# A fused attention and FFN kernel: how the second square layer's weight sums are fetched, summed and stored

## The chip, the core and the metric

The kernel runs on one core of one Trainium2 chip. The metric is device time in microseconds, lower is better. The engines are named as in the profile: PE (TensorE), DVE (VectorE), ACT (ScalarE), POOL (GpSimd) and SP (SyncE, which here only issues DMAs). "L846" is line 846 of the kernel before.

## The reference

x has the shape 2 x 2048 x 256. With a causal softmax attention of one head and a gated FFN of two square layers of 1024:

```python
xn = layernorm(x)
attn = softmax(causal(xn@Wq @ (xn@Wk).T) / 16) @ (xn@Wv) @ Wo
h = silu(xn@w1.T * s1) * (xn@w2.T * s2)     # 256 -> 1024
h = gelu(h@h1.T * sh1)                      # 1024 -> 1024, the first square layer
h = gelu(h@h2.T * sh2)                      # 1024 -> 1024, the second square layer
out = x + attn + h@w3.T * s3                # 1024 -> 256
```

All is float32. The FFN's weights are -1, 0 or 1 in the inputs; the kernel looks at them at run time and takes a branch of its own for such weights.

## The kernel before

The kernel has two parts. The first 280 us compute the attention and, beside it, examine the weights. Its results and the normalized, transposed x are stored to DRAM (`r_d`, `xT_d`). Then `ffn_ternary` works through N = 8 blocks of 512 rows in pairs, n = 0, 2, 4, 6.

Each square layer is a product of 1024 x 1024 weights with a pair of blocks of 1024 rows, done by a scheme of seven products of half size in place of eight (`STEPS`). Each step has a weight factor and an activation factor: step 0 is A11 with B11, step 1 S1 with T1, step 2 S2 with T2, step 3 S4 with B22, step 4 S3 with T3, step 5 A12 with B21, step 6 A22 with T4. The A are quarters of the weights; the S are sums of quarters. In the names of the code, S1 = a21 + a22, S2 = S1 - a11, S4 = a12 - S2 and S3 = a11 - a21.

A factor is a DRAM slab of 1 MB (`factors["h1"]` and `factors["h2"]`, seven slabs each, in the order of the steps). `fetch_factors` (L949) loads one into one of three SBUF buffers (pool `wpt`, on SP) as soon as a buffer is free, so that a factor is asked for two steps ahead of its use. `product` (L846) then runs 32 matmuls of 128 x 128 x 512.

The first layer's sums are made in the attention part. The second layer's are made in the FFN part, once, during the first pair (n = 0), by `make_h2(c)` for four chunks c = 0 to 3: two fetches of 512 KB on POOL's DMA queue (L915) into two tiles of the tag `stg`, four subtractions or additions of 128 x 512 on POOL (`sums_of_factors`, L151) into the one tile of the tag `sums` (`bufs=1`), and a store of 1 MB on POOL's queue (L919). `copy_h2` (L928, SP) copies the three plain quarters from DRAM to DRAM. `load_w3` fetches and rounds the last weights in two halves (L923, L132), in tiles of the tag `stg`. Where these calls stand is told by the dictionary `later`: names ("B11", "B21", ...) are quarters of the gated layer, numbers are steps of the first square layer:

```python
later = {
    "B11": lambda: make_h2(0), "B21": lambda: make_h2(1), "B12": lambda: copy_h2(0),
    0: lambda: copy_h2(5), 1: lambda: make_h2(2), 2: lambda: copy_h2(6),
    3: lambda: make_h2(3), 5: lambda: load_w3(0), 6: lambda: load_w3(SC // D),
}
```

`rests_of(n)` loads the attention's results (L962) and x (L963) of both blocks and adds them on POOL (L964); the outputs go into the same tiles and from there to DRAM (L999). x uses the tag `sums`, the two rests use the tag `stg`, one tile each.

The text's order is a priority only: the program is built with `schedule_with_timeline_sim=True`, a planner that gives each engine its order by a simulated timeline and adds the waits. On the chip each engine, and each queue of DMA issues (SP's, POOL's, ACT's), then runs in that fixed order.

Other lines that are named below: L170 the gated layer's products, L178 and L179 its activation (ACT) and scaling (DVE), L183 and L184 the split of an activation factor into two parts (ACT and DVE), L821, L826 and L827 the sums that make T1, T3 and T2 (DVE, POOL, DVE), L885 the sum for T4 (POOL), L866 and L867 the sums behind the products and their Gelu, L767 the loads of x.

Of the kernel before, what the change touches and what calls it, by code (L numbers as in the profile page):

```python
# [9 lines left out]
F32 = mybir.dt.float32  # L10
# [5 lines left out]
ALU = mybir.AluOpType  # L16
# [4 lines left out]
P = 128  # L21
TB = 512
NT = TB // P
# [13 lines left out]


STEPS = [("A11", "B11"), ("S1", "T1"), ("S2", "T2"), ("S4", "B22"), ("S3", "T3"), ("A12", "B21"), ("A22", "T4")]
LOW_BITS = 0xFFF  # L40


# [20 lines left out]
def attn_ffn_kernel(  # L63
# [35 lines left out]
    nc = tc.nc  # L99
    B, S, D = x.shape  # L100
# [4 lines left out]
    HC = H // P  # L105
    SC = 1024
# [15 lines left out]
    HB = H // 2  # L122
    HK = HC // 2
    factors = {k: dram.tile([P, len(STEPS), HK, HB], F32, name=f"factors_{k}") for k in ("h1", "h2")}

# [4 lines left out]
    def rounded(dst, src):  # L130

        nc.gpsimd.tensor_scalar(dst, src, 1.0, 0.0, ALU.mult, ALU.add)  # L132

    def rows_of(n):
        return x[n // NB, ds((n % NB) * TB, TB), :].rearrange("(t p) d -> p t d", p=P)
# [4 lines left out]
    def sums_of_factors(sums, halves, which, engine=nc.gpsimd):  # L140

        (a11, a21), (a12, a22) = ((t[:, :HB], t[:, HB:]) for t in halves)
        done = sums.bitcast(F32) if sums.dtype == F32R else sums
        for i in which:
            x, y, op = (
                (a21, a22, ALU.add),
                (done[:, 0, :], a11, ALU.subtract),
                (a12, done[:, 1, :], ALU.subtract),
                (a11, a21, ALU.subtract),
            )[i]  # L150
            engine.tensor_tensor(sums[:, i, :], x, y, op)  # L151
# [35 lines left out]
    with ExitStack() as actx:  # L187
        cp = actx.enter_context(tc.tile_pool(name="cp", bufs=1))
        stgp = actx.enter_context(tc.tile_pool(name="stgp", bufs=2))
# [360 lines left out]
        def low(tiles, dst):  # L550
# [4 lines left out]
            with tc.issue_after(marks["DVE"]):  # L555
                nc.vector.tensor_scalar(tb, tb, LOW_BITS, None, ALU.bitwise_and)
            with tc.issue_after(marks["ACT"]):
# [11 lines left out]
        sums = xh0.rearrange("p c h t -> p (c h) t")  # L569
# [180 lines left out]
    def ffn_ternary(actx):  # L750
# [4 lines left out]
        stgp = actx.enter_context(tc.tile_pool(name="stgpt", bufs=2))  # L755
# [6 lines left out]
        w3_sb = fw.tile([P, HC, D], F32R, name="w3_sbt")  # L762
        xh1 = fw.tile([P, DC, 2, TB], F32R, name="xh1t")

        def load_xh(n):
            t = xh1 if n % 2 else xh0
            nc.sync.dma_start(out=t.bitcast(F32).rearrange("p c h t -> p (c h t)"), in_=xT_d[n])  # L767
# [64 lines left out]
        def square(layer, n, B, sets, last, beside):  # L832
# [6 lines left out]
            def product(step, out, start):  # L839
                right = STEPS[step][1]  # L840
                fetch_factors()
                w = factor_tiles.pop(0)
                for o in range(HK):
                    for c in range(HK):
                        for a in range(2):
                            nc.tensor.matmul(  # L846
                                out=out[o], lhsT=w[:, c, ts(o, P)], rhs=sets[right][c][:, a, :],
                                start=(start and c == 0 and a == 0), stop=(c == HK - 1 and a == 1),
                                skip_group_check=True,
                            )  # L850
                if step in beside:
                    beside.pop(step)()
# [55 lines left out]
                    t2(C, nxt, name, i)  # L908
            return C, nxt

        def make_h2(c):
            halves = []
            for k in (c, c + HK):
                t = stgp.tile([P, SC], F32, tag="stg", name=f"stgt_h2_{k}")
                nc.gpsimd.dma_start(out=t, in_=h2[:, k, :])  # L915
                halves.append(t)
            sums = stgp.tile([P, 4, HB], F32, tag="sums", name=f"sums_h2_{c}", bufs=1)
            sums_of_factors(sums, halves, range(4))
            nc.gpsimd.dma_start(out=factors["h2"][:, 1:5, c, :], in_=sums)  # L919

        def load_w3(c):
            t = stgp.tile([P, SC], F32, tag="stg", name=f"stgt_w3_{c}")
            nc.gpsimd.dma_start(out=t, in_=w3[:, c : c + SC // D, :].rearrange("p c d -> p (c d)"))  # L923
            rounded(w3_sb[:, c : c + SC // D, :].rearrange("p c d -> p (c d)"), t)

        def copy_h2(step):
            k, o = {0: (0, 0), 5: (HK, 0), 6: (HK, HB)}[step]
            nc.sync.dma_start(out=factors["h2"][:, step], in_=h2[:, ds(k, HK), ds(o, HB)])  # L928

        later = {
            "B11": lambda: make_h2(0), "B21": lambda: make_h2(1), "B12": lambda: copy_h2(0),
            0: lambda: copy_h2(5), 1: lambda: make_h2(2), 2: lambda: copy_h2(6),
            3: lambda: make_h2(3), 5: lambda: load_w3(0), 6: lambda: load_w3(SC // D),
        }
        assert HK == 4 and HC == 2 * SC // D


        factor_order = [  # L940
            (layer, n, step) for n in range(0, N, 2) for layer in ("h1", "h2") for step in range(len(STEPS))
        ]
        factor_tiles = []

        def fetch_factors():
            while factor_order and len(factor_tiles) < 3:
                layer, n, step = factor_order.pop(0)
                w = wp.tile([P, HK, HB], F32R, tag="w", name=f"w_{layer}_{n}_{STEPS[step][0]}")
                nc.sync.dma_start(  # L949
                    out=w.bitcast(F32).rearrange("p c o -> p (c o)"),  # L950
                    in_=factors[layer][:, step].rearrange("p c o -> p (c o)"),
                )
                factor_tiles.append(w)

        def rests_of(n):


            xt = stgp.tile([P, 2, NT, D], F32, tag="sums", name=f"xt_{n}", bufs=1)
            rests = {}
            for m in (n + 1, n):  # L960
                rests[m] = rest = stgp.tile([P, NT, D], F32, tag="stg", name=f"rt_{m}")
                nc.sync.dma_start(out=rest, in_=r_d[m].rearrange("p (t d) -> p t d", d=D))  # L962
                nc.sync.dma_start(out=xt[:, m - n], in_=rows_of(m))  # L963
                nc.gpsimd.tensor_tensor(rest, rest, xt[:, m - n], ALU.add)  # L964
            return rests

        load_xh(1)
        fetch_factors()

        for n in range(0, N, 2):  # L970
            B, sets = first(n)
            for i in range(HK):
                t2(B, sets, f"{n}", i)
            if n + 2 < N:
                load_xh(n + 2)
                load_xh(n + 3)
            B, sets = square("h1", n, B, sets, False, later)
            rests = {}
            B, sets = square("h2", n, B, sets, True, {3: lambda: rests.update(rests_of(n))})
            for m in (n + 1, n):  # L980
                rest = rests[m]
                h = sets["B11"] + sets["B21"] if m == n else sets["B12"] + sets["B22"]
                ys = banks(NT, m > n)

                late = HK if m == n else 0
                order = [(t, c) for t in range(2) for c in range(HC - late)]
                order += [(t, c) for t in range(2) for c in range(HC - late, HC)]
                order += [(t, c) for t in range(2, NT) for c in range(HC)]
                for t, c in order:
                    for a in range(2):  # L990
                        nc.tensor.matmul(  # L991
                            out=ys[t][:, :D], lhsT=h[c][:, a, ts(t, P)], rhs=w3_sb[:, c, :],
                            start=(c == 0 and a == 0), stop=(c == HC - 1 and a == 1),
                        )
                    if c == HC - 1:
                        y = op.tile([P, D], F32, tag="y", name=f"yt_{m}_{t}")
                        nc.vector.tensor_tensor(y, ys[t][:, :D], s3, ALU.mult)
                        nc.vector.tensor_tensor(rest[:, t, :], y, rest[:, t, :], ALU.add)
                        nc.sync.dma_start(out=out[m // NB, rows(m, t), :], in_=rest[:, t, :])  # L999
# [154 lines left out]

    some = nc.values_load(flag[0:1, 0:1], min_val=0, max_val=LOW_BITS * SC * P)
    with tc.If(some == 0) as cmp:
        with ExitStack() as fctx:
            ffn_ternary(fctx)
# [43 lines left out]
```

## Time and profile before

| what | value |
|---|---|
| time, median of three runs | 882.9 us (882.52 to 883.9) |
| profiled execution, its own time | 883.71 us |
| span in the profile | 881.8 us |
| busy: PE, DVE, ACT, POOL | 97%, 73%, 57%, 27% |
| mean granted TensorE clock | 0.989 |
| FFN part, from about 282 us: start of the second product in the first layer, pairs n = 0, 2, 4, 6 | 312.3, 474.6, 620.6, 766.5 us |

The time is that of the whole execution on the device; the span reaches from the first to the last instruction of the profile. A busy share is a mean over the span. The chain of waits goes back from the last instruction, at each step to what released it. The windows give each engine's busy time, the granted clock (PEclk, 1.00 is full speed) and the DMA load in a stretch. A timeline line has start, length, engine, line, operation and, in brackets, the idle time before it and what ended it.

### The profile page before, as it was taken

What the parts mean: (1) busy time and instruction counts of PE and PEld (TensorE: products, weight loads), DVE (VectorE), ACT (ScalarE), POOL (GpSimd) and SP (SyncE); (2) the same over time, 40 slices, a digit from 0 to 9 for tenths busy, and PEclk for the clock granted to TensorE, in tenths of its full rate; (3) what the DMA queues carried; (4) which work ended last, traced back from release to release, by engine and by line L of the source; (5) the groups of instructions that cost most, each with busy time, mean ns of one, the idle gap of its engine ahead of it and who ended that gap; (6) DMA issues with size and microseconds to landing.
All of it is one profiled execution on the core that took longest, in us unless ns stands there. A gap on an engine that the chain in (4) does not pass through costs nothing.

```text
span 881.8 us, 12244 instructions
## 1 busy us (share of the span) xinstructions
PE 851.1 (97%) x4280; PEld 720.4 (82%) x4280; DVE 645.6 (73%) x1127; ACT 499.6 (57%) x881; POOL 234.2 (27%) x190
## 2 busy tenths in 40 slices
PE   8999989999999999489999999999999999999997
PEld 5988778887888888378988888898888898888887
DVE  6698787886875897876486397569559658948764
ACT  3456555745655475447266576636657645556671
POOL 4012643101211574750133042024215002502300
PEclk9999999999999999889999999999999999999999
DMA  9876799775892977584334444433444331134411
GB/s 314 332 231 198 231 316 291 260 251 163 231 342 73 396 282 251 201 301 148 132 100 152 148 149 147 145 98 134 149 144 144 143 137 55 49 143 144 143 48 52
DMA packets 62822, 162.52 MB, mean 184 GB/s; under 512 B 6560, under 2 KB 36384, under 8 KB 53536
## 3 DMA queue, kind: packets, MB, share of 16 engines
q1 hardware_dynamic: 54752, 136.48, 44.7%
q10 hardware_dynamic: 5472, 15.73, 5.5%
q0 software_dynamic: 2528, 9.44, 3.1%
q8 instruction: 36, 0.59, 0.3%
q14 instruction: 34, 0.28, 0.1%
HBM read 120.21 MB, written 47.71 MB: 190 GB/s over the span
## 4 chain that ended last, share of the span: by engine, by line
PE 75%; DMA 10%; POOL 4%; DVE 4%; issue 4%; ACT 1%; SPq 1%; ACTq 0%; POOLq 0%; DVEq 0%
PE ps L846 20%; PE ps_own L846 20%; PE ps L170 7%; PE ps L399 6%; PE ps_own L170 6%; PE po L478 4%; DMA e<-d 3%; PE ps_own L991 3%; PE ps L991 3%; POOL sums_h L151 2%; PE po L483 2%; PE ps L371 2%; DMA d<-b 1%; DMA factors_h<-sums_h 1%; DMA stgt_h<-in_ffn_h_w 1%
## 5 line engine op out<-in xcount | busy, mean ns | idle before, releaser
L399 PE MATMUL ps<-k,q 128*128 128x512 f32 (+3 forms) x480 | 109.0, 366 | 2.5 <-DVE s L408 1.7
L399 PEld LDWEIGHTS ps<-k,q 128*128 128x128 f32 x480 | 81.5, 189 | 15.0 <-DVE s L408 2.1
L478 PE MATMUL po<-v,pT 128*128 128x512 f32 x272 | 79.1, 400 | 5.4 <-DVE r L497 3.7
L460 POOL TENSOR_TENSOR pT<-e,pT 128x512 fp32r<-128x512 f32 (+3 forms) x30 | 35.5, 1185 | 154.1 <-ACT pT L458 108.3
L867 ACT ACTIVATE k_h_u<-k_h_u,h_s_sb 128x512 f32<-128x512 f32 x64 | 46.0, 723 | 34.0 <-DVE k_h_u L866 33.3
L964 POOL TENSOR_TENSOR rt<-rt,xt 128x1024 f32<-128x1024 f32 x8 | 20.0, 2497 | 166.7 <-DMA rt<-r_d 62.2
L478 PEld LDWEIGHTS po<-v,pT 128*128 128x128 f32 x272 | 47.5, 189 | 13.5 <-issue 2.7
L458 ACT CAST pT<-e 128x512 fp32r<-128x512 f32 (+3 forms) x60 | 32.6, 573 | 43.5 <-DMA e<-d 31.3
L420 ACT ACTIVATE s<-s,low 128x1024 f32<-128x1024 f32 (+7 forms) x48 | 42.9, 896 | 23.7 <-DVE low L414 23.6
L826 POOL TENSOR_TENSOR k_h_u<-k_h_p,k_h_u 128x512 f32<-128x512 f32 x16 | 22.5, 1407 | 116.1 <-ACT q L183 102.5
L408 DVE TENSOR_SCALAR_CACHE_REDUCE s<-ps 128x512 f32<-128x512 f32 (+3 forms) x80 | 47.1, 599 | 3.7 <-PE ps L399 3.1
L483 PEld LDWEIGHTS po<-v,pT 128*128 128x128 f32 x272 | 42.5, 189 | 6.2 <-DVE pT L460 0.5
L483 PE MATMUL po<-v,pT 128*128 128x256 f32 x272 | 46.1, 283 | 0.0
L846 PE MATMUL ps<-h_h_T,w_h_S 128*128 128x512 f32 x128 | 31.8, 409 | 13.5 <-DMA w_h_S<-factors_h 13.5
L184 DVE TENSOR_TENSOR q<-k_h_u,q 128x512 fp32r<-128x512 f32 x32 | 44.2, 1411 | 0.1
L846 PEld LDWEIGHTS ps<-h_h_T,w_h_S 128*128 128x128 f32 x128 | 25.4, 200 | 19.4 <-DMA w_h_S<-factors_h 14.0
L290 DVE STREAM_TRANSPOSE b<-s 128x1024 f32<-128x1024 f32 (+3 forms) x30 | 33.6, 1127 | 8.8 <-ACT s L420 7.7
L460 DVE TENSOR_TENSOR pT<-e,pT 128x512 fp32r<-128x512 f32 x30 | 24.8, 828 | 19.2 <-ACT pT L458 15.2
L885 POOL TENSOR_TENSOR k_h_p<-f_h_B,k_h_p 128x512 f32<-128x512 f32 x16 | 32.5, 2061 | 16.3 <-DVE h_h_T L184 16.3
L867 ACT ACTIVATE k_h_p<-k_h_p,h_s_sb 128x512 f32<-128x512 f32 x32 | 23.1, 723 | 22.6 <-DVE k_h_p L866 22.5
L170 PE MATMUL ps<-xh,w_sb 128*128 128x512 f32 x144 | 35.8, 391 | 0.0
L826 POOL TENSOR_TENSOR f_w_B<-f_w_B,f_w_B 128x512 f32<-128x512 f32 x16 | 25.7, 1620 | 37.5 <-DVE f_w_B L179 37.4
(179 smaller groups left out, 2205.6 us busy)
## 6 DMA issues: line engine op xcount, KB each, us to landing
w_h_S<-factors_h SPq DMA_DIRECT2D x32, 1024.0 KB, 4.7
w_h_A<-factors_h SPq DMA_DIRECT2D x24, 1024.0 KB, 4.7
d<-b SPq DMA_DIRECT2D x18, 512.0 KB, 3.9
e<-d SPq DMA_DIRECT2D x72, 128.0 KB, 4.1
xT_d<-k SPq DMA_DIRECT2D x8, 1024.0 KB, 8.0
stg<-in_ffn_h_w ACTq DMA_DIRECT2D x16, 512.0 KB, 6.3
x<-in_attn_x SPq DMA_DIRECT2D x16, 256.0 KB, 6.4
factors_h<-xh SPq DMA_DIRECT2D x4, 1024.0 KB, 5.1
```

Source lines behind the costliest of these rows:

```text
L170: nc.tensor.matmul(out=p, lhsT=w[:, c, ts(o, P)], rhs=xh[:, c, a, :], start=(c == 0 and a == 0), stop=(c == DC - 1 and a == 1),)
L184: nc.vector.tensor_tensor(r[:, 1, :], f, r[:, 0, :].bitcast(F32), ALU.subtract)
L399: nc.tensor.matmul(out=ps[:, :w], lhsT=qs[n][:, c, a, ts(t, P)], rhs=ks[m][:, c, b, :w], start=(k == 0), stop=(m < n and k == 3 * DC - 1),)
L408: marks["DVE"] = nc.vector.tensor_scalar(st["s"][:, ds(at, w)], ps[:, :w], 1.0, None, ALU.mult, ALU.max, accum_out=st["tops"][:, m - first ...
L420: marks["ACT"] = nc.scalar.activation(st["s"][:, at], st["s"][:, at], AF.Exp, bias=low, accum_out=st["sums"][:, u // UK : u // UK + 1],).ins
L460: engine.tensor_tensor(lo, src, hi.bitcast(F32), ALU.subtract)
L478: nc.tensor.matmul(out=st["po"], lhsT=pT[:, 0, ts(j, P)], rhs=vs[m][:, j, :, :], start=(m == first and j == 0), stop=False,)
L483: marks["PE"] = nc.tensor.matmul(out=st["po"][:, 0, :], lhsT=pT[:, 1, ts(j, P)], rhs=vs[m][:, j, 0, :], start=False, stop=(m == n and j == ...
L826: nc.gpsimd.tensor_tensor(B["B12"][i], B["B22"][i], B["B12"][i], ALU.subtract)
L846: nc.tensor.matmul(out=out[o], lhsT=w[:, c, ts(o, P)], rhs=sets[right][c][:, a, :], start=(start and c == 0 and a == 0), stop=(c == HK - 1 ...
L867: nc.scalar.activation(C[k][o], r[o] if r else banks[o], AF.Gelu, scale=s[:, at : at + 1])
L991: nc.tensor.matmul(out=ys[t][:, :D], lhsT=h[c][:, a, ts(t, P)], rhs=w3_sb[:, c, :], start=(c == 0 and a == 0), stop=(c == HC - 1 and a == 1),)
```

## The change

The sums of a chunk are written over the weights from which they are made. A tile is now 128 x 4 x 512 (8 KB a partition) and holds both rows of a chunk: a11, a21, a12, a22. Four operations in an order that needs no other place leave S2, S3, S4 and S1 in it, and the tile is stored as it is; the slabs of `factors["h2"]` therefore lie in another order, which `SLOTS` undoes at the load. The pool has two such tiles, so two chunks are in work at a time, in the room of the two `stg` tiles and the `sums` tile of before.

The fetches of the chunks go from POOL's queue to SP's and are set apart from the sums (`fetch_h2`): those of chunks 0 and 1 stand ahead of the first factors, those of chunks 2 and 3 behind the quarters B12 and B22. `make_h2(2)` moves from step 1 to step 2, `copy_h2(0)` from B12 to B21. w3 is fetched in one piece on SP, at step 5. In `rests_of` both blocks' rests share one tile, and x of both another. The stores of the sums stay on POOL's queue.

```diff
+SLOTS = {"h1": range(7), "h2": (0, 4, 1, 3, 2, 5, 6)}
...
+        raw_h2 = {}
+        def staged(name):
+            return stgp.tile([P, 4, HB], F32, tag="stg", name=name)
+        def fetch_h2(c):
+            t = raw_h2[c] = staged(f"stgt_h2_{c}")
+            for i, k in enumerate((c, c + HK)):
+                nc.sync.dma_start(out=t[:, ts(i, 2), :], in_=h2[:, k, :].rearrange("p (i o) -> p i o", i=2))
         def make_h2(c):
-            halves = []
-            for k in (c, c + HK):
-                t = stgp.tile([P, SC], F32, tag="stg", name=f"stgt_h2_{k}")
-                nc.gpsimd.dma_start(out=t, in_=h2[:, k, :])
-                halves.append(t)
-            sums = stgp.tile([P, 4, HB], F32, tag="sums", name=f"sums_h2_{c}", bufs=1)
-            sums_of_factors(sums, halves, range(4))
-            nc.gpsimd.dma_start(out=factors["h2"][:, 1:5, c, :], in_=sums)
-        def load_w3(c):
-            t = stgp.tile([P, SC], F32, tag="stg", name=f"stgt_w3_{c}")
-            nc.gpsimd.dma_start(out=t, in_=w3[:, c : c + SC // D, :].rearrange("p c d -> p (c d)"))
-            rounded(w3_sb[:, c : c + SC // D, :].rearrange("p c d -> p (c d)"), t)
+            t = raw_h2.pop(c)
+            a11, a21, a12, a22 = (t[:, i, :] for i in range(4))
+            nc.gpsimd.tensor_tensor(a22, a21, a22, ALU.add)
+            nc.gpsimd.tensor_tensor(a21, a11, a21, ALU.subtract)
+            nc.gpsimd.tensor_tensor(a11, a22, a11, ALU.subtract)
+            nc.gpsimd.tensor_tensor(a12, a12, a11, ALU.subtract)
+            nc.gpsimd.dma_start(out=factors["h2"][:, 1:5, c, :], in_=t)
+        def load_w3():
+            t = staged("stgt_w3").rearrange("p i o -> p (i o)")
+            nc.sync.dma_start(out=t, in_=w3.rearrange("p c d -> p (c d)"))
+            for i in range(HC * D // SC):
+                rounded(w3_sb.rearrange("p c d -> p (c d)")[:, ts(i, SC)], t[:, ts(i, SC)])
...
         later = {
-            "B11": lambda: make_h2(0), "B21": lambda: make_h2(1), "B12": lambda: copy_h2(0),
-            0: lambda: copy_h2(5), 1: lambda: make_h2(2), 2: lambda: copy_h2(6),
-            3: lambda: make_h2(3), 5: lambda: load_w3(0), 6: lambda: load_w3(SC // D),
+            "B11": lambda: make_h2(0), "B21": lambda: (make_h2(1), copy_h2(0)), "B12": lambda: fetch_h2(2),
+            "B22": lambda: fetch_h2(3), 0: lambda: copy_h2(5),
+            2: lambda: (make_h2(2), copy_h2(6)), 3: lambda: make_h2(3), 5: load_w3,
         }
...
-                    in_=factors[layer][:, step].rearrange("p c o -> p (c o)"),
+                    in_=factors[layer][:, SLOTS[layer][step]].rearrange("p c o -> p (c o)"),
...
         def rests_of(n):
-            xt = stgp.tile([P, 2, NT, D], F32, tag="sums", name=f"xt_{n}", bufs=1)
+            xt, rt = (
+                staged(f"{k}_{n}").rearrange("p i (u d) -> p (i u) d", d=D) for k in ("xt", "rt")
+            )
             rests = {}
-            for m in (n + 1, n):
-                rests[m] = rest = stgp.tile([P, NT, D], F32, tag="stg", name=f"rt_{m}")
+            for i, m in enumerate((n + 1, n)):
+                rests[m] = rest = rt[:, ts(i, NT), :]
                 nc.sync.dma_start(out=rest, in_=r_d[m].rearrange("p (t d) -> p t d", d=D))
-                nc.sync.dma_start(out=xt[:, m - n], in_=rows_of(m))
-                nc.gpsimd.tensor_tensor(rest, rest, xt[:, m - n], ALU.add)
+                nc.sync.dma_start(out=xt[:, ts(i, NT), :], in_=rows_of(m))
+                nc.gpsimd.tensor_tensor(rest, rest, xt[:, ts(i, NT), :], ALU.add)
...
         load_xh(1)
+        for c in range(2):
+            fetch_h2(c)
         fetch_factors()
```

More of the change, by code (lines that the diff above doesn't have):

```diff
@@ L932, in ffn_ternary @@
         later = {
-            "B11": lambda: make_h2(0), "B21": lambda: make_h2(1), "B12": lambda: copy_h2(0),
-            0: lambda: copy_h2(5), 1: lambda: make_h2(2), 2: lambda: copy_h2(6),
-            3: lambda: make_h2(3), 5: lambda: load_w3(0), 6: lambda: load_w3(SC // D),
+            "B11": lambda: make_h2(0), "B21": lambda: (make_h2(1), copy_h2(0)), "B12": lambda: fetch_h2(2),
+            "B22": lambda: fetch_h2(3), 0: lambda: copy_h2(5),
+            2: lambda: (make_h2(2), copy_h2(6)), 3: lambda: make_h2(3), 5: load_w3,
         }
-        assert HK == 4 and HC == 2 * SC // D
+        assert HK == 4 and HC * D == 4 * HB
         factor_order = [
```

## The prediction

> **What bounds the kernel now.** I read the page's busy shares first: PE is busy for 97% of the span, so a gain has to come out of PE's few idle stretches or its slow ones. The groups by line name one such stretch, and PE's waits over the first half of the FFN give it as a single wait:
>
> ```profile
> L846 PE MATMUL ps<-h_h_T,w_h_S 128*128 128x512 f32 x128 | 31.8, 409 | 13.5 <-DMA w_h_S<-factors_h 13.5
> ```
> ```profile
> PE ps L846 <- DMA w_h_S<-factors_h: 13.5, 1, 13.5
> ```
>
> The windows around it show a second cost beside the idle time, the granted clock (after the five engines come PEclk, the DMA share and GB/s):
>
> ```profile
> 356.20:363.50 7.30, 7.30 (x33) 5.82 (x31) 4.87 (x3) 2.50 (x5) 7.22 (x6) 1.00 0.00 1
> 363.50:377.15 13.65, 0.11 (x1) 0.00 (x1) 13.65 (x11) 6.49 (x12) 10.54 (x10) 0.66 0.91 324
> 377.15:386.60 9.45, 9.45 (x33) 7.63 (x34) 7.70 (x5) 2.83 (x6) 7.93 (x5) 0.77 0.82 310
> ```
>
> The reader is to see PE empty from 363.5 to 377.15, and the product behind it taking 9.4 us where its neighbours take 7.25. This is step 1 of the second square layer (operand S1) in the first pair of blocks; the later pairs have no such wait. The chain of waits says what made S1 late:
>
> ```profile
> 329.37 1.62 POOL sums_h L151
> 330.99 0.52 POOL stgt_h L915
> 331.51 0.76 POOL factors_h L919
> 332.27 11.13 DMA stgt_h<-in_ffn_h_w
> ...
> 348.44 7.01 DMA factors_h<-sums_h
> ...
> 364.96 5.65 DMA factors_h<-sums_h
> ...
> 370.73 6.38 DMA w_h_S<-factors_h
> ...
> 377.15 9.57 PE ps L846 x32
> ```
>
> The four chunks run one behind another: POOL fetches, sums, stores, and may not begin the next sums before the store of the last has left the only sums tile (POOL's waits in 296 to 440: 13.8 us in two for the stores, 11.3 us in three for the fetches). S1 needs all four chunks; the last store lands at 370.6, its load at 377.1.
>
> **What the Trainium skill says.** SBUF — State Buffer, "Who interferes with whom": a VectorE instruction with two SBUF inputs contends with a GpSimd instruction that reads SBUF, and the later one waits for the whole of the other. The trace agrees; DVE's timeline beside POOL's sums (298.65 to 303.88) and L826 (307.03 to 309.57) has
>
> ```profile
> 298.65 0.68 DVE L184 TENSOR_TENSOR h_T<-b,h_T 128x512 fp32r<-128x512 f32 x1
> 300.96 1.77 DVE L821 TENSOR_TENSOR b<-f_w_B,b 128x512 f32<-128x512 f32 x1
> 306.21 0.74 DVE L179 SCALAR_TENSOR_TENSOR f_w_B<-ps,w_s_sb,f_w_B 128x512 f32<-128x512 f32 x1
> 306.88 3.26 DVE L184 TENSOR_TENSOR h_B<-f_w_B,h_B 128x512 fp32r<-128x512 f32 x1
> ```
>
> where 0.68 is the undisturbed time, and L179, which reads PSUM, keeps its 0.74. DMA: Bandwidth & Descriptors, "Anatomy of one DMA", says that a wait is done by the issuing sequencer before dispatch: what stands behind a waiting fetch on SP waits with it. The trace agrees (SP stood 24.8 us at L962 for w3). TensorE: Matmul & The Clock Gate, "What's actually happening", has the clock fall after an idle window and rise after a busy one: here 0.66, 0.77, then 1.00.
>
> **The change part by part.**
>
> *PE's stall.* Without the wait S1 starts 7.25 after step 0, at 363.44, and ends at 370.7; its successor starts at 386.56 now. That is 15.87 us: 13.7 of waiting and 2.2 of clock. To be free of it, the last store must land early enough for the load (median 4.7 us) before 363.4, so by 358.7.
>
> *When the stores land after.* Removed from POOL: eight L915 issues (0.55 each) and two w3 issues (0.53). Added to SP: eight fetches and one w3 load, at 0.33 each about 3 us, on a queue mostly idle in the trace. The first four fetches leave SP at about 284 to 287, behind xh1t. The DMA rate in 284 to 305 is 391 GB/s, 2.7 us a MB: chunk 0 lands at about 291, chunk 1 at 293.5 (two us for completion). The sums keep number and shape, 4 x 1.62 = 6.5 us a chunk (row L151, 1.3 to 1.8 each): chunk 0 in 291 to 297.5, chunk 1 in 298.3 to 305, each followed by a 0.8 us store issue. No page states a price of writing in place; L826 does so in 1.27 to 1.83, the same band, so I take nothing (bounds 1.27 and 1.83 an operation: -1.4 and +0.8 a chunk, against the 10 us of slack below). The first store of before took the longest, 15.2 us; with that the two land at 313 and 321, and chunks 2 and 3 are fetched into their tiles by 322 and 329. POOL is held until about 325 by L826 and L885, then makes chunks 2 and 3 by 339, with stores landing at 341 to 349. That is 10 us before the deadline. S1's load waits for a buffer, free when A12 ends at 349.0, and is in by 355.
>
> *First factors.* SP's two MB of fetches go ahead of A11, S1 and S2. A11 is the fourth MB: 284 + 4 x 2.7 + 2 = 297, needed at 304.8; S1 and S2 at 300 and 303, needed at 312 and 319. Cost nothing, with A11's 8 us as cover; at half the rate A11 would land at 307.6, 3 us late.
>
> *The price: DVE.* Making chunk 1 moves from 324 to 331, where DVE had slack, into 298 to 305, where it has none. DVE is without idle from 294.4 to 330. PE's second output tile of A11 may start only when L179 has read its bank at 306.95, and it starts at about 306.9; step 2 waits 0.7 us (0.37 lost) for T2 already. Between 298.65 and 303.88 POOL's 5.07 us of sums cost DVE 0.44 + 1.09 + 0.33 = 1.86 over its undisturbed times, 0.37 per us. Another 6.5 us of sums cost 2.4; DVE's gap of 0.34 at 294 and the earlier chunk 0 return part. I take 2.0 us. Bounds: 6.5 (every us of POOL blocks DVE) and -0.4 (the waits on T2 go as well, two POOL issues less).
>
> *T2 of the second layer* comes next after the stall: DVE ends it at 376.4 now, and step 2 will want it at 370.7. It follows L826, which POOL starts at 360.7 because the sums hold it; in the second pair, without them, T2 is ready 5.1 us early (527.5 against 532.66). Freed of the last sums, POOL has two roundings of w3 (1.0 to 1.4 each) in front. I take nothing; bound +5.
>
> *The rest.* Both blocks' residuals now share a tile, so the next pair's load waits for all eight output stores, near 442 rather than 433; its sums are needed some 125 us later. The three copies have no producer and keep their early place. The one-piece w3 is used at 423. Nothing, within 0.3 either way.
>
> Sum against the profiled execution (883.71; span 881.8, 1.9 around it): -15.87 + 2.0 = -13.9, 869.8. The median shown is 882.9, 0.8 less, so 869.0.
>
> **The rivals.**
>
> *The stall only changes its cause (0.08).* SP now also carries the residual loads, and rt's tile is w3's, so rt must wait for the rounding on POOL. If rt stands before S1 on SP and POOL takes L826 first, S1 leaves at about 370 as now: SP's 24.8 us at L962 ended at 368.6, just before the store. Against it: w3 can be fetched at 341, and POOL is free then. Time: 880 to 884.
>
> *SP blocked by its own fetch (0.09), the one that is slower.* The fetch of chunk 3 waits for chunk 1's store, and the S4 factor stands behind it. If POOL makes chunk 1 after L885 as it does now (324 to 331), that store lands at 340, S4 leaves at 340 instead of 312.5 and lands at about 347 behind chunk 3's MB: PE, due at 327.2, stops for 19.8 us and pays 2.2 of clock. Net 882.9 - 15.9 + 22.0 = 889.0. It decides from the moment when S4 leaves later than about 320. For it: SP's queue is in order, and POOL's order in the trace had chunk 1 there. Against it: in the trace the first tile was refetched only at 303.8, so chunk 1 could not come earlier; now both chunks are in at 294.
>
> *A smaller new stall (0.15).* T2 in either layer or S4 late by 3 to 6 us: 871 to 875.
>
> **How the numbers follow.** The main case has 0.68: 866.5 to 871, by DVE's bounds, 869.0 taken. With the smaller stall it makes 0.83; the range 866.4 to 874.5 holds these less their tails. About 0.2% (1.8 us) is what a measurement of this kernel can tell from no change. Faster: 0.68 + 0.15 + part of the unchanged stall, 0.87; same: 0.04; slower: 0.09.
>
> **What would show it.** Right: no wait of PE on w_h_S near 363, the product there at 7.25; POOL with eight sums in a row by about 305 and eight more after L885; stores landing before 350; A11 or S2 some 2 us later than 305.05 and 319.56. Wrong: PE waiting for S4 near 327, SP standing at a chunk's fetch past 320, or POOL with chunk 1 behind L885; and for the DVE term, L184 and L821 in 295 to 320 at 0.68. The steady pairs keep 145.9 us each (467.61, 613.55, 759.49); if they move, the shared residual tile was mispriced.

## The result, and the profile after

The change makes the kernel faster: 870.7 us (median of 870.27 to 874.31) against 883.4 us (882.52 to 884.86) for the kernel before on the same chip, a ratio of 0.986 (95% interval 0.983 to 0.989). The forecast was 869.0 us. The profiled execution took 871.0 us, its span is 869.1 us, 12.7 less than before, and the mean granted clock is 0.993 in place of 0.989.

Line numbers after the change are two higher in the code above `make_h2`: the product is L848, DVE's scaling L181, its split L186, the sums for T1, T3 and T2 L823, L828 and L829, the sum for T4 L887. New are the fetch of a chunk (L922), its four sums (L928 to L931) and its store (L932); the factor load is L963, the loads of the rests and of x L978 and L979, their addition L980.

The stall is gone. The windows around the place where S1 used to hang (after the stretch and its length come PE, PEld, DVE, ACT and POOL, then PEclk, DMA share, GB/s):

```profile
345.00:362.00 17.00, 17.00 (x77) 14.09 (x76) 15.42 (x17) 10.63 (x18) 9.43 (x7) 1.00 0.96 363
362.00:371.00 9.00, 9.00 (x42) 7.45 (x41) 9.00 (x12) 5.76 (x11) 4.16 (x2) 1.00 0.54 202
371.00:382.00 11.00, 11.00 (x50) 9.14 (x49) 11.00 (x8) 10.23 (x21) 9.36 (x5) 1.00 0.51 189
```

PE is busy for the whole of each stretch, at PEclk 1.00, where before it lay idle for 13.5 us (PEclk 0.66 in that stretch) and then ran at 0.77. PE's waits from 280 to 475 us are now of another kind and small:

```profile
PE ps L848 <- DVE f_w_B L181: 1.2, 2, 1.0
PE ps L848 <- DVE h_T L186: 0.6, 1, 0.6
```

**The first price lies in the first pair.** PE's timeline of A11 and of the end of S2 in the first layer:

```profile
304.36 2.65 PE L848 MATMUL ps<-q,w_h_A 128*128 128x512 f32 x11
...
310.26 3.25 PE L848 MATMUL ps<-q,w_h_A 128*128 128x512 f32 x13 [0.99 <-DVE f_w_B L181]
...
322.99 5.96 PE L848 MATMUL ps<-h_T,w_h_S 128*128 128x512 f32 x25 [0.64 <-DVE h_T L186]
```

A11 begins at 304.36 and S1 behind it at 313.35: 8.99 us for a product that takes 7.25. S2 runs from 320.60 to 328.79, 8.19. DVE's timeline shows why it was late, and POOL's what stood beside it:

```profile
299.06 1.78 DVE L186 TENSOR_TENSOR h_T<-b,h_T 128x512 fp32r<-128x512 f32 x1
...
303.00 1.77 DVE L823 TENSOR_TENSOR b<-f_w_B,b 128x512 f32<-128x512 f32 x1
304.70 0.74 DVE L181 SCALAR_TENSOR_TENSOR f_w_B<-ps,w_s_sb,f_w_B 128x512 f32<-128x512 f32 x1
305.46 0.69 DVE L186 TENSOR_TENSOR h_T<-b,h_T 128x512 fp32r<-128x512 f32 x1
```
```profile
298.55 1.74 POOL L929 TENSOR_TENSOR stgt_h<-stgt_h 128x512 f32<-128x512 f32 x1
...
302.60 1.63 POOL L931 TENSOR_TENSOR stgt_h<-stgt_h 128x512 f32<-128x512 f32 x1
...
339.83 0.77 POOL L932 DMA_DIRECT2D factors_h<-stgt_h  x1 [0.30 <-POOL stgt_h L931]
```

The reader is to see L186 and L823 at 1.8 us while a sum stands beside them, L186 back at 0.69 when the sums have ended at 304.2, and L181, which reads PSUM, at 0.74 throughout. The last store of a chunk is issued at 339.8; before, it was issued at 364.96.

**The second price lies in the later pairs.** The starts of the first layer's S1 are 313.35, 460.85, 607.46 and 753.90 us: periods of 146.6 and 146.4 between the later pairs, where before they were 145.9. In each of them A11 waits a little for DVE, as here on PE's timeline; from 453.20 to 460.85 us that product takes 7.65, where it took 7.23 before:

```profile
458.51 2.34 PE L848 MATMUL ps<-q,w_h_A 128*128 128x512 f32 x9 [0.17 <-DVE f_w_B L181]
```

Some 28 us earlier POOL adds both blocks' rests back to back, and DVE's splits beside it take 1.74 each (POOL's timeline, then DVE's):

```profile
430.83 5.25 POOL L980 TENSOR_TENSOR rt<-rt,xt 128x1024 f32<-128x1024 f32 x2 [50.47 <-DMA xt<-in_attn_x]
```
```profile
430.33 3.48 DVE L186 TENSOR_TENSOR q<-b,q 128x512 fp32r<-128x512 f32 x2
```

From 433.74 to 460.80 DVE is busy for 26.96 of 27.06 us, so that it comes late to A11. In the kernel before, the two additions stood apart (437.25, 2.40 us, and 445.45, 2.87 us). They are together now because both blocks' x are loaded together, into the tile that the last output store leaves (SP's waits):

```profile
SPq L979 <- DMA out<-rt: 1.2, 1, 1.2
```

**The sum.** The attention part isn't touched, and its end moves from run to run (A11 began at 303.6 to 306.8 in the runs of this study). So I count from the start of A11 to the end of the span: 576.75 before, 564.74 after, 12.01 less. That is 15.87 (the stall and its slow clock) less 2.31 in the first pair (A11 1.74, S2 0.94, less the 0.37 that S2 lost before) less 1.55 in the later pairs (about 0.5 each). A11's own start was 0.69 earlier, which makes the span's 12.7.

### The profile page after: what moved, and what is told of

It is laid out like the page before. It is cut to its first block, busy times and chain, and to the rows that moved or that the text cites. A ratio compares the mean times of both kernels' runs of the same rounds, so it can differ in the third digit from the quotient of the medians.

```text
span 869.1 us, 12231 instructions
## 1 busy us (share of the span) xinstructions
PE 851.9 (98%) x4280; PEld 720.8 (83%) x4280; DVE 645.9 (74%) x1127; ACT 498.6 (57%) x881; POOL 236.1 (27%) x180
## 4 chain that ended last, share of the span: by engine, by line
PE 83%; DVE 7%; DMA 5%; issue 2%; ACT 2%; SPq 1%; POOL 0%; ACTq 0%; DVEq 0%; POOLq 0%
PE ps_own L848 23%; PE ps L848 22%; PE ps L401 8%; PE po L480 5%; PE ps L172 5%; PE ps_own L172 4%; PE ps_own L1009 4%; PE ps L1009 4%; PE po L485 3%; PE ps L357 2%; DMA e<-d 2%; PE ps L373 2%; DVE f_w_B L181 1%; DMA stg<-in_ffn_w_w 1%; DVE h_T L186 1%
## 5 line engine op out<-in xcount | busy, mean ns | idle before, releaser
L980 POOL TENSOR_TENSOR rt<-rt,xt 128x1024 f32<-128x1024 f32 x8 | 21.5, 2698 | 165.1 <-issue 114.6
L480 PEld LDWEIGHTS po<-v,pT 128*128 128x128 f32 x272 | 48.4, 192 | 12.1 <-issue 2.7
L828 POOL TENSOR_TENSOR k_h_u<-k_h_p,k_h_u 128x512 f32<-128x512 f32 x16 | 23.2, 1453 | 125.5 <-ACT q L185 108.8
L186 DVE TENSOR_TENSOR q<-k_h_u,q 128x512 fp32r<-128x512 f32 x32 | 45.9, 1462 | 0.0
L887 POOL TENSOR_TENSOR k_h_p<-f_h_B,k_h_p 128x512 f32<-128x512 f32 x16 | 34.4, 2181 | 21.2 <-DVE h_h_T L186 21.2
L828 POOL TENSOR_TENSOR f_w_B<-f_w_B,f_w_B 128x512 f32<-128x512 f32 x16 | 27.0, 1705 | 32.4 <-DVE f_w_B L181 32.4
L868 DVE TENSOR_TENSOR k_h_u<-ps_own,k_h_u 128x512 f32<-128x512 f32 x32 | 21.7, 686 | 18.5 <-PE ps_own L848 18.5
L848 PE MATMUL ps<-q,w_h_A 128*128 128x512 f32 x128 | 31.7, 395 | 1.9 <-DVE f_w_B L181 1.7
```

The source lines that it names most:

```text
L186: nc.vector.tensor_tensor(r[:, 1, :], f, r[:, 0, :].bitcast(F32), ALU.subtract)
L480: nc.tensor.matmul(out=st["po"], lhsT=pT[:, 0, ts(j, P)], rhs=vs[m][:, j, :, :], start=(m == first and j == 0), stop=False,)
L828: nc.gpsimd.tensor_tensor(B["B12"][i], B["B22"][i], B["B12"][i], ALU.subtract)
L848: nc.tensor.matmul(out=out[o], lhsT=w[:, c, ts(o, P)], rhs=sets[right][c][:, a, :], start=(start and c == 0 and a == 0), stop=(c == HK - 1 ...
```

## The experiments

Each was compared with the kernel before on its own chip; "from A11 to the end" is the stretch just defined. e1 to e4 ran on one chip, e5 to e8 on another; the kernel before took 883.2 us on the first and 883.7 us on the second. Each figure of that stretch comes from one profiled execution.

### e1: the sums of chunk 1 left out

Chunk 1's slabs then hold raw weights; fetches and stores stay.

```diff
-            nc.gpsimd.tensor_tensor(a22, a21, a22, ALU.add)
...
+            if c != 1:
+                nc.gpsimd.tensor_tensor(a22, a21, a22, ALU.add)
...
```

> Chunk 1's four sums are left out: it is stored as fetched, and all else is as in the changed kernel. Theory (POOL's sums of chunk 1 hold DVE up where it has no slack, and PE waits for DVE in A11 and in S2): PE's waits of 0.99 us in A11 and 0.64 us in S2 of the first pair go, the two products fall from 9.0 and 8.2 us to 7.3 and at most 7.6, and the time is about 2.3 us below the changed kernel, near 868.4. Rival (the waits come from the transfers, whose traffic is the same here, or from DVE's own work): both waits stay, and the time is that of the changed kernel within 0.5 us.

Measured: 868.8 us (868.42 to 871.91), ratio 0.985 (0.983 to 0.988). PE's timeline has A11 whole:

```profile
304.08 7.42 PE L848 MATMUL ps<-q,w_h_A 128*128 128x512 f32 x32
```

S1 follows at 311.34 and S2 at 318.59, 7.25 apart, and S2 too is clean. From A11 to the end it takes 562.92, 1.82 less than after the change. That is less than the 2.68 of A11 and S2: from the start of S2 to the end of S3 it is 22.53 in place of three times 7.25, 21.76, with a wait on the load of S4, which PE, now early, meets before it has landed (0.2 of idle time); and the later pairs wait as they did. It follows that the delay of A11 and S2 is made by the four sums of chunk 1.

### e2: the chunks fetched on POOL's queue

```diff
-                nc.sync.dma_start(out=t[:, ts(i, 2), :], in_=h2[:, k, :].rearrange("p (i o) -> p i o", i=2))
+                nc.gpsimd.dma_start(out=t[:, ts(i, 2), :], in_=h2[:, k, :].rearrange("p (i o) -> p i o", i=2))
```

> The changed kernel, but the fetches of the four chunks are issued by POOL and not by SP. Theory (what frees the stall is that two chunks are in work at once; SP's part is that a fetch can leave without waiting for its turn on POOL): POOL's order now has the fetches of chunks 2 and 3 behind its sums and ahead of the stores, so the last store lands later than 347, by the length of one fetch and one store, at about 360 to 366, and PE waits for S1 again by 3 to 9 us: 873 to 880. DVE's cost in A11 is smaller, since chunk 1's sums come later. Rival (the queue doesn't matter): no wait on S1, 870 to 871.

Measured: 878.9 us (872.14 to 883.14), ratio 0.995 (0.993 to 0.998). The mechanism that I expected was wrong: PE doesn't wait for S1 at all. Its waits from 280 to 475 us are above all for T2, in both layers:

```profile
PE ps L848 <- DVE h_T L186: 2.9, 1, 2.9
PE ps_own L848 <- DVE h_h_T L186: 2.7, 2, 1.8
```

S2 takes 12.1 us in the first layer and 13.4 in the second, against 8.2 and 7.25 after the change; A11 is clean. From A11 to the end it is 9.2 longer. Where PE waits in the first layer, POOL's timeline shows chunk 1's sums among L887, while DVE makes T2; the last store comes 12.7 us later than after the change:

```profile
315.16 1.75 POOL L928 TENSOR_TENSOR stgt_h<-stgt_h 128x512 f32<-128x512 f32 x1
316.86 1.74 POOL L887 TENSOR_TENSOR f_w_B<-f_w_B,f_w_B 128x512 f32<-128x512 f32 x1
...
352.50 0.78 POOL L932 DMA_DIRECT2D factors_h<-stgt_h  x1 [0.30 <-POOL stgt_h L931]
```

In the second layer three of DVE's splits for T2 take 6.25 us, in place of 1.88 after the change (369.41), and beside them POOL runs L887 and adds rests (DVE's timeline, then POOL's):

```profile
373.15 6.25 DVE L186 TENSOR_TENSOR h_h_T<-k_h_p,h_h_T 128x512 fp32r<-128x512 f32 x3
```
```profile
374.34 2.83 POOL L980 TENSOR_TENSOR rt<-rt,xt 128x1024 f32<-128x1024 f32 x1
```

After the change that addition began at 372.40, when T2 was done. The late store doesn't explain the wait: T2's first sum (L829), which comes behind L828, began at 366.73, 1.5 us later than after the change, but S1, ahead of S2, began 2.4 later. Both causes are read from the timelines and weren't tested by themselves. What is shown: the tiles alone, with the fetches left on POOL, give only 0.5%, and the planner put the sums in another place.

### e3: the kernel before, with its fetches on SP

```diff
-                nc.gpsimd.dma_start(out=t, in_=h2[:, k, :])
+                nc.sync.dma_start(out=t, in_=h2[:, k, :])
```

> The kernel before with one edit: the chunks are fetched by SP in place of POOL; the two halves and the one tile of sums stay. Theory (the single tile of sums and the two halves set the pace, and the order of chunk, store, chunk stays): the stall at S1 keeps at least 9 of its 13.5 us; time 879 to 884. Rival (POOL's queue made the fetches late, in place or not): the stall falls below 4 us; time 868 to 873.

Measured: 887.0 us (882.94 to 891.91, 20 runs), ratio 1.005 (1.003 to 1.006): slower, and above the 879 to 884 that I expected. The profiled run, 884.38 us, is one of the fastest of the twenty, so its trace doesn't show the whole of the loss. The stall on S1 stays (PE's timeline):

```profile
378.16 9.19 PE L846 MATMUL ps<-h_h_T,w_h_S 128*128 128x512 f32 x32 [11.53 <-DMA w_h_S<-factors_h]
```

SP's timeline shows the rival "SP blocked by its own fetch" at work, at a small price:

```profile
328.08 0.33 SPq L915 DMA_DIRECT2D stgt_h<-in_ffn_h_w  x1
328.51 0.38 SPq L949 DMA_DIRECT2D w_h_S<-factors_h  x1
```

SP stood 13.3 us at a fetch (until 328.08) for a tile that POOL was still reading, with the load of S3 behind it. S1 began 74.0 us after A11, 1.9 later than before. This is what the Trainium skill says in DMA: Bandwidth & Descriptors, "Anatomy of one DMA": the issuing sequencer waits, not the DMA engine. POOL's sums waited 22.1 us for stores to leave the one sums tile. So moving the fetches alone doesn't help while the sums need a place of their own. With e2: the new tiles take the stall away, and the gain needs both parts.

### e4: one tile a block for the rests

Each block's rest and x share a tile, in place of both rests in one and both x in the other.

```diff
-            xt, rt = (
-                staged(f"{k}_{n}").rearrange("p i (u d) -> p (i u) d", d=D) for k in ("xt", "rt")
-            )
...
-                rests[m] = rest = rt[:, ts(i, NT), :]
+                xr = staged(f"xr_{m}").rearrange("p i (u d) -> p (i u) d", d=D)
+                rests[m] = rest = xr[:, :NT, :]
...
-                nc.sync.dma_start(out=xt[:, ts(i, NT), :], in_=rows_of(m))
+                nc.sync.dma_start(out=xr[:, NT:, :], in_=rows_of(m))
...
```

> The changed kernel, with the two residual tiles cut the other way: one tile for a block's rest and its x, the other for the other block's. Theory (in the changed kernel both adds of 2.6 us run back to back just when the next pair's gated layer starts, since x's tile comes free only with the last output store; DVE gets 2 us late and PE waits for it in A11 of pairs 2, 4 and 6): one block's tile is free four stores earlier, the adds come apart, PE's waits in A11 of the later pairs (0.7 us at PE, 2.0 at the weight loads) go, and the pairs take 145.9 to 146.1 us in place of 146.4 to 146.6: about 1.5 us less, near 869.2. Rival (the later pairs are slower for another reason, such as the first pair's end): their period stays at 146.4 to 146.6.

Measured: 870.3 us (868.54 to 872.3), ratio 0.985 (0.983 to 0.988). The periods of the later pairs are 145.9 again, PE has no wait there, and POOL's additions stand apart on its timeline:

```profile
425.74 2.53 POOL L978 TENSOR_TENSOR xr<-xr 128x1024 f32<-128x1024 f32 x1 [44.39 <-DMA out<-xr]
433.20 2.40 POOL L978 TENSOR_TENSOR xr<-xr 128x1024 f32<-128x1024 f32 x1 [4.93 <-DMA xr<-in_attn_x]
```

The first pair keeps its waits (1.0, 0.6 and 0.4). From A11 to the end it takes 563.30, 1.44 less than after the change: the second price comes from the tiles that the two blocks share. Its median hardly shows that, since A11 began 0.7 later in the profiled run.

### e5: the sums of chunk 1 behind L887

Chunk 1 gets the room that w3 takes later, so that its sums needn't free a tile early. The sums of chunks 1 and 2 then stand behind the last L887 of the first layer, which the code keeps as `marks["POOL"]`; `issue_after` puts what follows behind it.

```diff
...
-            t = raw_h2[c] = staged(f"stgt_h2_{c}")
+            t = staged(f"stgt_h2_{c}") if c != 1 else fw.tile([P, 4, HB], F32, tag="w3", name="stgt_h2_1")
+            raw_h2[c] = t
...
+        def made_late(*cs):
+            with tc.issue_after(marks["POOL"]):
+                for c in cs:
+                    make_h2(c)
...
-            "B11": lambda: make_h2(0), "B21": lambda: (make_h2(1), copy_h2(0)), "B12": lambda: fetch_h2(2),
-            "B22": lambda: fetch_h2(3), 0: lambda: copy_h2(5),
-            2: lambda: (make_h2(2), copy_h2(6)), 3: lambda: make_h2(3), 5: load_w3,
+            "B11": lambda: make_h2(0), "B21": lambda: (fetch_h2(2), copy_h2(0)), "B12": lambda: fetch_h2(3),
+            0: lambda: copy_h2(5),
+            2: lambda: (made_late(1, 2), copy_h2(6)), 3: lambda: make_h2(3), 5: load_w3,
...
```

> The changed kernel with chunk 1 in a third place (the room of the w3 tile, which is free until w3 is rounded) and its sums behind POOL's L887 of the first pair; chunks 2 and 3 get the two other tiles early, so no fetch waits for chunk 1's store. Theory (what is left of the loss in A11 and S2 is chunk 1's sums beside DVE's busiest stretch, and it is a matter of when): A11 takes 7.25, S2 at most 7.6; three chunks of sums run on POOL in about 323 to 344, the last store lands by about 354, S1 doesn't wait; from the start of A11 to the end 562.4 us in place of 564.7. Rival (the twelve late sums come too late, or hold DVE up in the splits of B21 and T4): A11 and S2 are clean, but PE waits for S1 or for A12 or A22 by 2 us or more, and nothing is won.

Measured: 868.4 us (867.12 to 871.15), ratio 0.983 (0.981 to 0.986). All products of the first layer take 7.25 in the first pair, and from A11 to the end it is 562.11, 2.63 less than after the change (A11's 1.74 and S2's 0.94 make 2.68). The sums contend with DVE in their new place too, without PE noticing: twelve of them end at 341.2 and the last store is issued at 341.5. DVE's timeline and POOL's, side by side:

```profile
321.14 6.88 DVE L186 TENSOR_TENSOR h_h_B<-f_w_B,h_h_B 128x512 fp32r<-128x512 f32 x4
```
```profile
320.63 3.44 POOL L929 TENSOR_TENSOR stgt_h<-stgt_h 128x512 f32<-128x512 f32 x2
```

Both engines take 1.72 us for each instruction. The contention is still there, but it falls where DVE has slack.

### e6 and e7: both prices removed

e6 is e5 with e4. e7 is e5 with the additions of the rests put behind the last L887 of the second layer:

```diff
-                nc.gpsimd.tensor_tensor(rest, rest, xt[:, ts(i, NT), :], ALU.add)
+                with tc.issue_after(marks["POOL"]):
+                    nc.gpsimd.tensor_tensor(rest, rest, xt[:, ts(i, NT), :], ALU.add)
```

> The edits of the last two together: chunk 1's sums late, and one residual tile for each block. Theory (the two losses lie in different stretches and add up): from the start of A11 to the end 564.7 - 2.3 - 1.4 = 561.0 us, a time near 867. Rival (one hides the other): no better than 562.4.

> Chunk 1's sums late, the residual tiles as in the changed kernel, and the residual adds put behind POOL's L887 of the second square layer, far from the gated layer. Theory (what slows the later pairs is when the adds run, not in which tile they are): the periods of pairs 2, 4 and 6 are 145.9 as with a tile for each block, the whole 561.0 us from A11 on. Rival (it is the tile's release by the output stores that slows the pairs, through SP's queue): the periods stay at 146.4 to 146.6.

Measured: e6 867.7 us (865.56 to 869.24), ratio 0.982 (0.979 to 0.984); e7 866.1 us (865.47 to 867.31), ratio 0.980 (0.978 to 0.983). In both, PE has no wait from 280 us on in the list of its waits, the later periods are 145.9, and from A11 to the end they take 560.52 and 560.43, 4.2 to 4.3 less than after the change; 2.68 and 1.55 make 4.23. e7's additions on POOL's timeline:

```profile
372.72 5.66 POOL L989 TENSOR_TENSOR rt<-rt,xt 128x1024 f32<-128x1024 f32 x2
```

They still stand back to back, but where PE doesn't wait for DVE. Between e6 and e7, the profiled runs differ almost in the attention part alone (A11 at 305.48 and 304.17). e7 has the lowest median of this study; its interval overlaps that of e6 and lies below that of the change as given.

### e8: chunk 1's sums replaced by fills

The output of each of the four operations is filled with 1.0, in place of the sum, to tell a sum's reads from its writes.

```diff
+            if c == 1:
+                for a in (a22, a21, a11, a12):
+                    nc.gpsimd.memset(a, 1.0)
+            else:
...
```

> The changed kernel with chunk 1's four sums replaced by four fills of the same 128x512 pieces with a constant: POOL is busy in the same place, but reads nothing from SBUF. Theory (DVE is held up by POOL's reads of SBUF and not by POOL being busy): DVE's two-input instructions beside the fills take their 0.68 us, A11's wait goes, as where the sums are left out. Rival (any work of POOL on SBUF, writes too, holds DVE up): DVE's instructions beside the fills are stretched to 1 us and more, and A11 keeps a wait in proportion to the fills' length.

Measured, one run: 870.6 us, with A11 at 306.76, 2.4 later than after the change. A11 and S2 are clean, and from A11 to the end it takes 562.14, 2.60 less than after the change. POOL's timeline and DVE's:

```profile
298.53 1.00 POOL L930 MEMSET stgt_h<- 128x512 f32 x2
```
```profile
297.63 1.51 DVE L186 TENSOR_TENSOR h_T<-b,h_T 128x512 fp32r<-128x512 f32 x1
299.07 0.68 DVE L823 TENSOR_TENSOR b<-f_w_B,b 128x512 f32<-128x512 f32 x1
```

L823 keeps its 0.68 beside a fill (298.53 to 299.53), while L186 takes 1.51 beside a sum (297.29 to 298.59). That agrees with the Trainium skill (SBUF — State Buffer, "Who interferes with whom"), which has DVE's second input contend with GpSimd's reads and not with its writes. But a fill takes 0.5 us in place of a sum's 1.3 to 1.7, so that the fills would have cost little in any case. The experiment is weak on that point, and I don't rest the reading on it.

## Why the prediction was right, and where it was off

- **The stall: as forecast, 15.87.** The forecast put S1 at 363.44; it began at 365.06, which is 363.44 less A11's earlier start (0.69) plus the 2.31 that the first pair lost. The chunk was in place early: the load was issued at 350.74, when the end of A12 (350.7) had freed its buffer.
- **The stores: as forecast.** I had them issued by 339 and landing at 341 to 349; the last was issued at 339.8 and had landed by 348.7, when SP was released from it. Where I had one chunk's sums after the other's, POOL mixed them (L928 of chunk 1 at 295.16, ahead of L931 of chunk 0), and both were done at 304.2. The operations in place took 1.29 to 1.76 us, the band that I took from L826.
- **The first factors: nothing, as forecast.** A11's wait is for DVE, and PE waits for no factor's load.
- **DVE's price: 2.31 where 2.0 was taken.** The place and the mechanism were right (e1 and e5), the term was 0.3 too small. Its rate, 0.37 us of DVE for each of POOL's sums' us, left out chunk 0's first sum (294.90, 1.29 us), beside which L184 took 1.63, 0.95 over its 0.68. With it, 6.36 us of sums cost DVE 2.81, or 0.44 a us; after the change, eight sums of 12.36 us cost it 5.55, or 0.45 a us. At such a rate a chunk costs 2.9, an estimate from these figures; PE lost 2.68, of which S2 had lost 0.37 before. That the 0.4 which I took off for DVE's gap and the earlier chunk 0 comes to S2's 0.37 is chance. The main case's upper end doesn't follow from DVE's bound either: 869.0 - 2.0 + 6.5 is 873.5, not 871.
- **T2 of the second layer: nothing, but barely.** DVE ended it at 371.29 and S2 began at 372.31: 1.0 us to spare, where the second pair of before had 5.1. In e2, PE waits there.
- **"The rest. Nothing, within 0.3 either way": wrong, 1.55.** This step failed. I asked when the sums of the rests are needed (125 us later) and not what making them does to DVE. The tile for x becomes free only with the last output store, so that both additions run back to back at the start of the next pair's gated layer, and they hold DVE up there as the sums do in the first pair. It is the same mechanism that I had priced two paragraphs above. e4 and e7 remove it in two ways, and e6 and e7 account for all of it. The forecast did name the sign: if the steady pairs move, the shared tile was mispriced.
- **The total.** -15.87 + 2.31 + 1.55 is -12.01; forecast was -13.9. Added to that, the attention part ended 0.69 earlier, which is chance: by that luck the profiled execution missed its forecast (871.0 against 869.8) by 1.2 and not by 1.9.
- **The rivals.** "The stall only changes its cause" had the right order and the wrong time. SP's timeline after the change:

```profile
313.54 0.32 SPq L963 DMA_DIRECT2D w_h_S<-factors_h  x1
313.96 2.76 SPq L922 DMA_DIRECT2D stgt_h<-in_ffn_h_w  x4
...
348.73 0.80 SPq L978 DMA_DIRECT2D rt<-r_d  x2
350.74 0.32 SPq L963 DMA_DIRECT2D w_h_S<-factors_h  x1
```

The loads of the rests do stand ahead of S1 on SP, and they did wait:

```profile
SPq L978 <- DMA factors_h<-stgt_h: 3.4, 1, 3.4
```

They waited for a store, not for w3's rounding, and left 1.8 us before S1's buffer was free, so it cost nothing. "SP blocked by its own fetch" didn't come: S4 left at 313.54, ahead of the fetches of chunks 2 and 3, and SP stood only 1.1 us for them, because POOL had made chunk 1 ahead of L828. e3 shows that the mechanism exists.

## What to carry to other kernels

Work in place can free the room for a second piece in work: here that took the wait for the only sums tile out of the chain (e2), which moving the fetches alone didn't (e3), and the sums themselves took no longer. Whether a second sums tile, without working in place, would do the same wasn't tried. When work moves on POOL, look up what DVE does in the same microseconds and whether it is late there; the same sums cost PE 2.7 us in one place and nothing some 25 us later (e5). Ask this of every piece that moves, the small ones too: a shared tile that only puts two additions side by side cost 1.55 us, where the large move cost 2.31.

## What the runs showed of the hardware

- Where POOL and DVE both read two SBUF inputs without a gap, neither keeps its pace: in e5 eight splits of 128x512 on DVE and eight sums on POOL took 1.72 us each, where they take 0.68 and 1.28 to 1.30 undisturbed. So POOL, too, takes a third longer. The two overlap in part: 0.68 and 1.29 make 1.97, more than 1.72.
- SP is not always free to issue. Three copies of 1 MB from DRAM to DRAM, issued one behind another, held SP for 8.5 us (L942 at 288.48) where the three factor loads just ahead of them took 1.2 us; one of the copies took 6.3 us to issue. No run here tells what sets this.
- In the kernel before, the product that follows 13.5 us without work is slow: 9.4 us in place of 7.25, at PEclk 0.77. In e3 the same product took 9.0 (378.16 to 387.19) after 11.5 us of waiting, at 0.80.
